# A post-norm layer on one core: the order of work ahead of its branch and in its closing stretch

## The chip, the cores and the metric

The kernel runs on one core of a Trainium2 chip. The core has a matrix engine (TensorE, PE in the profile, with PEld for its weight loads), VectorE (DVE), ScalarE (ACT), GpSimd (POOL), SyncE (SP, which here only issues DMAs) and 16 DMA engines. The metric is the time of one execution in device microseconds; the median of three runs is what the change is compared with.

## The reference

The input is x, 4 batches of 2048 tokens of 256 values. A gated linear attention of 16 heads (64 wide) and then a small "coupled" feed-forward follow, each with a residual and a layer norm.

```python
xn = _layer_norm(x, ln_gamma, ln_beta)
Q, K, V = xn @ WQ.T + bQ, xn @ WK.T + bK, xn @ WV.T + bV
gate = silu(xn @ Wg.T + bg);  alpha = sigmoid(alpha_logit)
h = alpha * h + k[:, None] * v[None, :];  o = q @ h          # step by step over the tokens, per head
x = layernorm(x + (x + (o * gate) @ WO.T + bO))

gf = global_net(x.mean(axis=1))                              # one number per batch
out = x
for _ in range(3):                                           # cycles 0, 1, 2
    tf = coupling_net(out)                                   # gelu, gelu, gelu, sigmoid; one number per token
    coupling = 0.1 + adaptive_range * (0.7 * gf + 0.3 * tf - 0.5) * 2
    out = out + coupling * twist(out)
x = layernorm(x + out)
```

`twist` permutes and negates quarters of a token's 256 values, and twisting twice gives the negative. So the kernel does not carry `out` through the cycles: it carries u = W1 applied to out and v = W1 applied to twist(out), and a cycle is u + c v and v - c u, with c the coupling of each token.

## The kernel before

**Stages.** First the constants are loaded and a few tables are made from the decay alpha: `up` and `down` (its powers, doubled step by step), `kf` and `qf` (what keys and queries are scaled by), `dtok` (decays by token), `bVt` (the bias of the values, repeated over the partitions). The first group of 512 tokens is normalised into `xn0` and its first values `V0` are made. A `flag` says whether the decays and weights lie in a safe range. Every engine reads the flag (line 1329) and branches: `program(True)` is the fast program, which these inputs take.

**The fast program** works through 4 batches of 4 groups of 512 tokens (`its` adds 8 head pairs to each). For each head pair it projects K, Q and gate, forms scores, updates of the state and products; between these pieces the function `between` slips in steps of three queues: `posts` (output projection and norm of a finished group), `nets` (the global net) and `couples` (the coupled feed-forward of two groups). A step is one piece of a Python generator, up to its next `yield step(...)`, with an engine and an estimated time that serve only to choose what is slipped in.

**Order on the engines.** The first stage and the fast program stand inside `tc.manual_schedule(engines=ORDERED)`: PE, DVE, ACT and POOL execute in the order in which the Python code issues, each on its own queue, and wait on each other through semaphores. What the last batch still has open after the last head pair is run by `the_end()`, which reads `AT_THE_END` letter by letter: `o` is the next step of a post, `n` of the global net, `p` of the couple of groups 0 and 1, `q` of the couple of groups 2 and 3, and `v` of `first_twisted`, which makes v for that second couple.

**The first stage around the change.** `double(i)` (VectorE) needs `powers[0]`, the sigmoid of the logit (ACT, line 257). In program order the doublings 0 to 2 stand between the statistics and the normalisation `xh` of the first group (line 159); the transposes of xh (line 182) and ACT's copies into `xn0` (line 184) follow, then the values (`values_of`: two matmuls, line 199, and an add on VectorE, line 203). The flag needs the largest of several squares, one of which is of the largest value of wQ (`peak`, line 295, a reduction of 128x2048 on VectorE), by way of `high`, `most`, `small`, `good`, and a matmul with ones (line 308). Values 3, two groups of transposes and ACT's two copies into `dtok` (line 324) end the stage. A PSUM bank there is one of four (`bank`).

**A couple's steps in the last batch** are: the first layer (line 823), layer 2 (line 905), layer 3 (line 940), layer 4 and tanh into `cs` (lines 949 and 952). Then for cycles 1 and 2 and for both halves s: `turn`, which scales `cs` into c (line 868), sends its first row through DRAM to get c by token (`by_token`, SP's DMAs), and updates; `gelu` (line 899) and layer 2; then layers 3 and 4. After cycle 2 the last tanh is by token (lines 957 and 959), the output's coefficients are worked out on VectorE with one power on POOL (lines 970 to 993), and the output is made by ACT (`own`, line 1002) and VectorE (`twisted`, line 1016) and stored.

In cycle 1 of the last batch VectorE and POOL share the update: VectorE makes c v (line 875) and adds it into u (line 878), POOL makes c u (line 876) and subtracts it from v (line 880):

```python
for o, (t0, t1) in enumerate(ts):
    nc.vector.tensor_mul(t0, cs[s], v[s][:, o, :])
    nc.gpsimd.tensor_mul(t1, cs[s], u[s][:, o, :])
```

`SPARE` holds four 128x512 buffers for each couple, which are no longer in use by then (a half of the values for the first, the tiles A and carry for the second). Cycle 2 uses VectorE alone and updates u only.

Of the kernel before, what the change touches and what calls it, by code (L numbers as in the profile page):

```python
# [42 lines left out]
F32 = mybir.dt.float32  # L43
I32 = mybir.dt.int32
U8 = mybir.dt.uint8
AF = mybir.ActivationFunctionType
# [23 lines left out]

AT_THE_END = "qoopooqnnqnpqppvppqvqqqpqppqqpqqpqppqpppppqqqpqpqqqqpqpqpppqqpqpppqpppqqqpqqqqqq"
STAGES = ((2, 4), (8, 4), (32, 2))
# [6 lines left out]
def post_norm_layer(ctx: ExitStack, tc: tile.TileContext, a: dict, out: bass.AP):  # L79
# [152 lines left out]
    with ExitStack() as first:  # L232
# [4 lines left out]
        def bank():  # L237
            return psum.tile([P, 512], F32, tag="pf", name="pf")


        diag = work.tile([P, HP, P], F32, tag="diag", name="diag")
# [13 lines left out]
        nc.vector.memset(high, 0.0)  # L255
        powers = [work.tile([P, HP, 1], F32, tag=f"apow{i}", name="apow") for i in range(C.bit_length())]
        nc.scalar.activation(powers[0], logit.unsqueeze(2), AF.Sigmoid)

# [32 lines left out]
        square(4, w_in["K"].rearrange("p k o -> p (k o)"))  # L291
        values_of(bank(), xn0, V0, 0, 0)

# [4 lines left out]
        nc.vector.tensor_mul(high[:, 5:6], peak, peak)  # L298
        values_of(bank(), xn0, V0, 0, 1)
        most = work.tile([P, 1], F32, tag="most", name="most")  # L300
# [4 lines left out]
        nc.vector.scalar_tensor_tensor(good, low, LOW_ALPHA, small, ALU.is_ge, ALU.mult)  # L305
        values_of(bank(), xn0, V0, 0, 2)
        pt = bank()
        nc.tensor.matmul(pt[0:1, 0:1], good, ones[:, 0:1], start=True, stop=True)
# [6 lines left out]
        values_of(bank(), xn0, V0, 0, 3)  # L315
        for half in range(2):
            hps = slice(half * (HP // 2), (half + 1) * (HP // 2))
            pt = bank()
            for j in range(HP // 2):
                nc.tensor.transpose(  # L320
                    pt[:, j * P : (j + 1) * P],
                    two[:, half * (HP // 2) + j].rearrange("p c s -> p (c s)"), ident,
                )
            nc.scalar.copy(dtok[:, hps, :].rearrange("p j i -> p (j i)"), pt)  # L324

# [9 lines left out]
    def layer(fast, inside):  # L335
# [335 lines left out]
        def step(kind, time, ready=always, act=0.0, delay=0.0, at=None):  # L671
            return kind, time, ready, act, delay, at
# [111 lines left out]
        def feed_forward(b, g0):  # L784
# [20 lines left out]
            u, v = [], []  # L805
            h1, h2 = {}, {}
            done = {}

# [52 lines left out]
            def first_twisted():  # L861
                for s in range(2):
                    yield from first(s, w1j, v, "v")

            def turn(s, cycle):

                yield step("dve", 0.75, lambda: b in shift and len(v) == 2, at=lambda: max(done["cs"], shift[b][1]))
                nc.vector.tensor_scalar(cs[s], cs[s], ar3, shift[b][0], ALU.mult, ALU.add)
                by_token(s, cycle - 1)
                if cycle == 1 and end:  # L870

                    done["u", s] = yield step("dve", 2.6)
                    ts = [(new("t"), SPARE[g0].pop(0)) for o in range(2)]
                    for o, (t0, t1) in enumerate(ts):
                        nc.vector.tensor_mul(t0, cs[s], v[s][:, o, :])
                        nc.gpsimd.tensor_mul(t1, cs[s], u[s][:, o, :])
                    for o, (t0, t1) in enumerate(ts):
                        nc.vector.tensor_add(u[s][:, o, :], u[s][:, o, :], t0)
                    for o, (t0, t1) in enumerate(ts):
                        nc.gpsimd.tensor_sub(v[s][:, o, :], v[s][:, o, :], t1)  # L880
                    return
                for o in range(2):
                    done["u", s] = yield step("dve", 1.3)
                    uo, vo = u[s][:, o, :], v[s][:, o, :]
                    t0 = new("t")
                    nc.vector.tensor_mul(t0, cs[s], vo)
                    if cycle == 1:
                        t1 = new("t")
                        nc.vector.tensor_mul(t1, cs[s], uo)
                        done["u", s] = yield step("dve", 1.3)  # L890
                    nc.vector.tensor_add(uo, uo, t0)
                    if cycle == 1:
                        nc.vector.tensor_sub(vo, vo, t1)

            def gelu(s):
                done["h1", s] = yield step("act", 1.4, delay=0.2, at=lambda: done["u", s])
                for o in range(2):
                    h1[s, o] = new("h1")
                    nc.scalar.activation(h1[s, o], u[s][:, o, :], AF.Gelu, bias=b1[:, o : o + 1])

# [22 lines left out]
            for cycle in range(3):  # L923
                if cycle and end:
                    for s in range(2):
                        yield from turn(s, cycle)
                    for s in range(2):
                        yield from gelu(s)
                        yield from layer2(s)
                elif cycle:  # L930
                    for s in range(2):
                        yield from turn(s, cycle)
                        yield from gelu(s)
# [433 lines left out]
```

## Time and profile before

| what | value |
|---|---|
| median of three runs | 1835.79 us (1835.6 to 1835.98) |
| the profiled execution | 1836.18 us, of which the span is 1834.4 us |
| TensorE busy | 1781.6 us, 97% of the span |
| VectorE busy | 1348.1 us, 73% |
| ScalarE busy | 755.7 us, 41% |
| GpSimd busy | 499.5 us, 27% |
| mean granted TensorE clock | 0.994 |
| first projection of the fast program (line 480) | begins at 24.97 us |
| last matmul of the program (line 957) | 1817.79 us and 1.05 us |
| last VectorE instruction | begins at 1829.07 us |

The profile is of one execution. A line such as `L878 DVE TENSOR_TENSOR u<-u,t 128x512 f32<-128x512 f32 x4 | 6.9, 1755 | 0.0` names the line of the kernel, the engine, the operation, the tile written and those read, the shape, the number of instructions, then their busy time in microseconds, the mean of one in nanoseconds and the idle time before them. The chain of work that ended last is followed back from the end: each piece is what released the next one. A window row gives the stretch, its length, the busy time of PE, PEld, VectorE, ACT and POOL with their instructions, the granted clock of TensorE, the share of the DMA engines and GB/s.

### The profile page before, as it was taken

The page shows a single profiled execution, that of the slowest core. Times are in us where ns is not written, and L with a number is a line of the kernel's source. Part 1 is how long each engine was busy: PE and PEld are TensorE (multiplying, and loading weights), DVE is VectorE, ACT ScalarE, POOL GpSimd, SP SyncE. Part 2 cuts the span into 40 slices and gives each one's busy share as a digit, 9 for nine tenths or more (in the row PEclk, how much of TensorE's full clock was granted, in tenths as well). Part 3 has the DMA queues.
Part 4 walks back from the last instruction along what each step waited for, and adds up shares of the span by engine and source line. Part 5 has one row for each costly group of instructions (what it writes and reads, how often), then busy time and mean ns, then how long its engine had stood idle before and what let it go on. Part 6 is the DMA issues. An engine that isn't in the chain of part 4 may idle for free.

```text
span 1834.4 us, 47983 instructions
## 1 busy us (share of the span) xinstructions
PE 1781.6 (97%) x20894; PEld 1026.4 (56%) x20894; DVE 1348.1 (73%) x3099; ACT 755.7 (41%) x1226; POOL 499.5 (27%) x452
## 2 busy tenths in 40 slices
PE   7999999999999999999999999999999999999985
PEld 3655555566555555565555555565555555555541
DVE  5677775767887868877688776877668876777467
ACT  3222324322454434543354334553355433453545
POOL 1332232223233222233132222222222232222242
PEclk9999999999999999999999999999999999999997
DMA  4000000000001000010001100010000100000002
GB/s 166 2 2 25 2 25 2 1 25 2 25 14 36 24 13 13 25 36 14 24 2 36 36 2 25 2 48 25 1 25 2 47 25 2 2 4 22 24 2 60
DMA packets 43819, 39.69 MB, mean 22 GB/s; under 512 B 20912, under 2 KB 39216, under 8 KB 43600
## 3 DMA queue, kind: packets, MB, share of 16 engines
q1 hardware_dynamic: 42320, 36.25, 6.2%
q8 instruction: 166, 2.72, 0.6%
q14 instruction: 53, 0.43, 0.1%
q10 hardware_dynamic: 1280, 0.29, 0.1%
HBM read 21.26 MB, written 15.27 MB: 20 GB/s over the span
## 4 chain that ended last, share of the span: by engine, by line
PE 89%; DVE 9%; issue 1%; ACT 1%; DMA 0%; POOL 0%; DVEq 0%; ACTq 0%
PE pj L480 34%; PE pj L683 12%; PE pj L199 11%; PE sc L573 4%; PE pj L905 4%; PE pu L1144 4%; PE pu L1161 4%; PE pj L630 4%; PE pj L847 3%; PE sc L646 3%; PE pj L940 1%; DVE states L656 1%; PE pj L823 1%; PE pj L949 1%; PE pj L710 1%
## 5 line engine op out<-in xcount | busy, mean ns | idle before, releaser
L526 POOL TENSOR_TENSOR qd<-QA,up 128x512 f32<-128x512 f32 x128 | 164.3, 1284 | 1159.6 <-ACT QA L498 1107.5
L494 ACT ACTIVATE KT<-pj,bK 128x512 f32<-128x512 f32 x128 | 87.9, 687 | 471.2 <-PE pj L480 471.2
L480 PE MATMUL pj<-xn,wK 128*128 128x512 f32 x512 | 253.8, 618 | 0.8 <-ACT dtok L324 0.8
L480 PE MATMUL pj<-xn,wg 128*128 128x512 f32 x512 | 240.6, 592 | 0.0
L480 PE MATMUL pj<-xn,wQ 128*128 128x512 f32 x512 | 240.6, 592 | 0.0
L656 DVE SCALAR_TENSOR_TENSOR states<-states,up,sc 128x64 f32<-128x64 f32 x768 | 215.8, 281 | 27.4
L199 PE MATMUL pj<-wV,xn 128*128 128x512 f32 x496 | 233.4, 593 | 0.0
L683 PE MATMUL pj<-wO,og 128*128 128x256 f32 x1024 | 231.9, 379 | 1.5 <-DVE og L1174 1.5
L683 PEld LDWEIGHTS pj<-wO,og 128*128 128x128 f32 x1024 | 194.3, 190 | 54.2 <-issue 27.7
L635 DVE TENSOR_TENSOR KE<-pj,dtok 128x512 f32<-128x512 f32 x128 | 88.1, 689 | 175.5 <-PE pj L630 175.5
L536 POOL TENSOR_TENSOR QF<-QA,qf 128x512 f32<-128x512 f32 x128 | 175.0, 1367 | 0.0
L480 PEld LDWEIGHTS pj<-xn,wQ 128*128 128x128 f32 x512 | 97.3, 190 | 122.4 <-issue 120.8
L480 PEld LDWEIGHTS pj<-xn,wg 128*128 128x128 f32 x512 | 97.3, 190 | 122.4 <-issue 110.2
L589 ACT COPY A<-sc 32x256 f32<-32x256 f32 x256 | 92.4, 361 | 147.0 <-PE sc L573 143.8
L498 ACT ACTIVATE QA<-pj,bQ 128x512 f32<-128x512 f32 x128 | 87.9, 687 | 140.5 <-PE pj L480 140.5
L480 PEld LDWEIGHTS pj<-xn,wK 128*128 128x128 f32 x512 | 86.7, 189 | 70.7 <-issue 62.2
L1161 PEld LDWEIGHTS pu<-A,V 64*64 64x64 f32 x4096 | 71.4, 134 | 84.9 <-DVE A L594 41.2
L199 PEld LDWEIGHTS pj<-wV,xn 128*128 128x128 f32 x496 | 84.6, 191 | 59.3 <-issue 59.3
L729 DVE TENSOR_TENSOR X<-pj,X 128x512 f32<-128x512 f32 x66 | 45.4, 688 | 96.9 <-PE pj L683 96.9
L510 ACT ACTIVATE gate<-pj,bg 128x512 f32<-128x512 f32 x128 | 88.0, 688 | 67.2 <-PE pj L480 62.7
L1174 DVE TENSOR_TENSOR og<-pu,gate 64x256 f32<-64x256 f32 x256 | 108.0, 422 | 6.3
L203 DVE TENSOR_TENSOR V<-pj,bVt 128x512 f32<-128x512 f32 x124 | 85.3, 688 | 34.4 <-PE pj L199 34.1
(222 smaller groups left out, 2721.2 us busy)
## 6 DMA issues: line engine op xcount, KB each, us to landing
X<-in_x SPq DMA_DIRECT2D x15, 512.0 KB, 3.8
out<-y SPq DMA_DIRECT2D x28, 256.0 KB, 2.1
kept<-X SPq DMA_DIRECT2D x13, 512.0 KB
x<-kept SPq DMA_DIRECT2D x13, 512.0 KB, 3.4
wV<-in_WV SPq DMA_DIRECT2D x1, 1024.0 KB, 6.2
wK<-in_WK SPq DMA_DIRECT2D x1, 1024.0 KB
wQ<-in_WQ SPq DMA_DIRECT2D x1, 1024.0 KB, 6.6
wg<-in_Wg SPq DMA_DIRECT2D x1, 1024.0 KB
```

Of the source, the lines that this page charges most:

```text
L199: nc.tensor.matmul(ps, xnT[:, k, i * P : (i + 1) * P], w_in["V"][:, k, half * 512 : (half + 1) * 512], start=(k == 0), stop=(k == KD - 1),)
L480: nc.tensor.matmul(ps, w_in[n][:, k, hp * P : (hp + 1) * P], xn[b, g][:, k, :], start=(k == 0), stop=(k == KD - 1),)
L494: nc.scalar.activation(kt, ps, AF.Identity, bias=b_in["K"][:, hp : hp + 1])
L510: nc.scalar.activation(gt, ps, AF.Silu, bias=b_in["g"][:, hp : hp + 1])
L526: nc.gpsimd.tensor_mul(qd, QA[it][:, :, 0:C], up[:, it[2], 1 : C + 1].unsqueeze(1).to_broadcast([P, NC, C]))
L536: nc.gpsimd.tensor_mul(qs[:, :, 0:C].rearrange("p c (n l) -> p c n l", l=H), qv.rearrange("p c (n l) -> p c n l", l=H), qf[:, hp, :].unsqu ...
L589: nc.scalar.copy(av[r, :, H:], pv[r, :, C : C + H])
L635: nc.vector.tensor_mul(ke, pt.rearrange("p (i x) -> p i x", i=NT), at(dtok, it[2], [P, NT, P]))
L656: nc.vector.scalar_tensor_tensor(o, before, up[:, hp, C : C + 1], u, ALU.mult, ALU.add)
L683: nc.tensor.matmul(ps[:, ii * D : (ii + 1) * D], og[b, g, hp][:, i * P : (i + 1) * P], wO[:, hp, :], start=(hp == hps[0]), stop=(hp == hps ...
L1161: tc.keep_in_program_order(nc.tensor.matmul(po[place(h, c), c, i * C : (i + 1) * C], V[r, i, m + h, :], A[r, h, i, :], start=False, stop=T ...
L1174: nc.vector.tensor_mul(ov[r, 1], pv[place(h, 1), 1], gv[r, 1])
```

## The change

Ahead of the branch:

- The sigmoid is the first instruction of the stage (ahead of the `diag` product and the copies into `bVt`).
- The adds and matmuls of values 1 stand with those of values 0, ahead of `peak`.
- The transposes and copies that make `dtok` stand ahead of the flag's matmul. The flag, `kf`, `qf` and values 3 follow.

In cycle 1 of the last batch:

- `turn` makes a new u in a `SPARE` buffer on VectorE alone: c v, then that plus u. POOL has no part in it. From then on `u_of` gives the new buffer.
- `turn_v`, a new step on VectorE behind layer 2 of both halves, multiplies the old u by c in its place and subtracts it from v.
- `AT_THE_END` lists the steps anew; it has two more `p` and two more `q`, for `turn_v`.

```diff
+        powers = [work.tile([P, HP, 1], F32, tag=f"apow{i}", name="apow") for i in range(C.bit_length())]
+        nc.scalar.activation(powers[0], logit.unsqueeze(2), AF.Sigmoid)
         diag = work.tile([P, HP, P], F32, tag="diag", name="diag")
...
-        powers = [work.tile([P, HP, 1], F32, tag=f"apow{i}", name="apow") for i in range(C.bit_length())]
-        nc.scalar.activation(powers[0], logit.unsqueeze(2), AF.Sigmoid)
...
-        values_of(bank(), xn0, V0, 0, 0)
+        for i in range(2):
+            values_of(bank(), xn0, V0, 0, i)
         peak = work.tile([P, 1], F32, tag="peak", name="peak")
...
-        values_of(bank(), xn0, V0, 0, 1)
...
         values_of(bank(), xn0, V0, 0, 2)
-        pt = bank()
-        nc.tensor.matmul(pt[0:1, 0:1], good, ones[:, 0:1], start=True, stop=True)
-        nc.vector.tensor_scalar(flag, pt[0:1, 0:1], P - 0.5, None, ALU.is_ge)
-
-        nc.vector.tensor_copy(kf[:, :, 0 : M + 1], down[:, :, C - M : C + 1])
-        nc.vector.tensor_copy(qf[:, :, M:H], up[:, :, 0:M])
-        nc.vector.reciprocal(kf[:, :, M + 1 : H], up[:, :, 1:M])
-        nc.vector.reciprocal(qf[:, :, 0:M], down[:, :, C - M : C])
-        values_of(bank(), xn0, V0, 0, 3)
         for half in range(2):
...
             nc.scalar.copy(dtok[:, hps, :].rearrange("p j i -> p (j i)"), pt)
+        pt = bank()
+        nc.tensor.matmul(pt[0:1, 0:1], good, ones[:, 0:1], start=True, stop=True)
+        nc.vector.tensor_scalar(flag, pt[0:1, 0:1], P - 0.5, None, ALU.is_ge)
+
...
+        values_of(bank(), xn0, V0, 0, 3)
...
-AT_THE_END = "qoopooqnnqnpqppvppqvqqqpqppqqpqqpqppqpppppqqqpqpqqqqpqpqpppqqpqpppqpppqqqpqqqqqq"
+AT_THE_END = "qoovoqonnpnppqpppvqpqpqpppqqpqqqpppqpppqppqpqqpqpqqqqpqqqpqpqqpqpqpqppqpppqpqqqqqqqq"
...
+            def u_of(s, o):
+                return new_u.get((s, o), u[s][:, o, :])
...
-                    done["u", s] = yield step("dve", 2.6)
-                    ts = [(new("t"), SPARE[g0].pop(0)) for o in range(2)]
-                    for o, (t0, t1) in enumerate(ts):
-                        nc.vector.tensor_mul(t0, cs[s], v[s][:, o, :])
-                        nc.gpsimd.tensor_mul(t1, cs[s], u[s][:, o, :])
-                    for o, (t0, t1) in enumerate(ts):
-                        nc.vector.tensor_add(u[s][:, o, :], u[s][:, o, :], t0)
-                    for o, (t0, t1) in enumerate(ts):
-                        nc.gpsimd.tensor_sub(v[s][:, o, :], v[s][:, o, :], t1)
+                    done["u", s] = yield step("dve", 2.8)
+                    for o in range(2):
+                        new_u[s, o] = SPARE[g0].pop(0)
+                        nc.vector.tensor_mul(new_u[s, o], cs[s], v[s][:, o, :])
+                        nc.vector.tensor_add(new_u[s, o], new_u[s, o], u[s][:, o, :])
                     return
...
+            def turn_v(s):
+
+                yield step("dve", 2.8)
+                for o in range(2):
+                    uo, vo = u[s][:, o, :], v[s][:, o, :]
+                    nc.vector.tensor_mul(uo, uo, cs[s])
+                    nc.vector.tensor_sub(vo, vo, uo)
...
                     for s in range(2):
                         yield from gelu(s)
                         yield from layer2(s)
+                    if cycle == 1:
+                        for s in range(2):
+                            yield from turn_v(s)
```

In steps, from the point where p's `cs` of cycle 0 is at hand, the new list runs: u of p; between its pieces the first layer of q; layer 2 of q and p; v of p; u of q; cycle 2 of p; v of q; cycle 2 of q; the coefficients and outputs of p and q.

More of the change, by code (lines that the diff above doesn't have):

```diff
@@ L324, in post_norm_layer @@
             nc.scalar.copy(dtok[:, hps, :].rearrange("p j i -> p (j i)"), pt)
+        pt = bank()
+        nc.tensor.matmul(pt[0:1, 0:1], good, ones[:, 0:1], start=True, stop=True)
+        nc.vector.tensor_scalar(flag, pt[0:1, 0:1], P - 0.5, None, ALU.is_ge)
+        nc.vector.tensor_copy(kf[:, :, 0 : M + 1], down[:, :, C - M : C + 1])
+        nc.vector.tensor_copy(qf[:, :, M:H], up[:, :, 0:M])
+        nc.vector.reciprocal(kf[:, :, M + 1 : H], up[:, :, 1:M])
+        nc.vector.reciprocal(qf[:, :, 0:M], down[:, :, C - M : C])
+        values_of(bank(), xn0, V0, 0, 3)
         nc.gpsimd.iota(trow, pattern=[[1, C]], base=0, channel_multiplier=0)
@@ L806, in feed_forward @@
             h1, h2 = {}, {}
+            new_u = {}
             done = {}
@@ L883, in turn @@
                     done["u", s] = yield step("dve", 1.3)
-                    uo, vo = u[s][:, o, :], v[s][:, o, :]
+                    uo, vo = u_of(s, o), v[s][:, o, :]
                     t0 = new("t")
@@ L898, in gelu @@
                     h1[s, o] = new("h1")
-                    nc.scalar.activation(h1[s, o], u[s][:, o, :], AF.Gelu, bias=b1[:, o : o + 1])
+                    nc.scalar.activation(h1[s, o], u_of(s, o), AF.Gelu, bias=b1[:, o : o + 1])
+            def turn_v(s):
[4 more added lines that the diff above has]
+                    nc.vector.tensor_sub(vo, vo, uo)
             def layer2(s):
```

## The prediction

> **What bounds the kernel now.** I read the chain of work that ended last first, because it says which stages can pay at all. On the page its shares are:
>
> ```profile
> PE 89%; DVE 9%; issue 1%; ACT 1%; DMA 0%; POOL 0%; DVEq 0%; ACTq 0%
> ```
>
> The long middle belongs to TensorE (PE) and its instruction stream is not touched. The change lies in the two ends, so I read those in the trace. For the first 45 us, the chain in order of time (start, length, engine and line; "xh" is the normalised X):
>
> ```profile
> 9.03 1.28 ACT L257
> 10.32 0.22 ACT apow L257
> 10.57 0.17 DVE up L262
> ...
> 11.66 0.33 DVE xh L159
> ...
> 17.64 2.20 DVE peak L295
> ...
> 24.71 0.18 ACT dtok L324
> 24.97 5.39 PE pj L480 x12
> ```
>
> The reader should see three things: a table load and the sigmoid hold VectorE (DVE) up to 10.57, since the doublings precede xh in its order (the wait rows give 2.8 us of idle there, released by apow); the reduction of wQ leads to the flag; and the first projection of the branch waits for the second dtok copy, which ends at 24.87.
>
> For the end I took busy time by window (length, PE, PEld, DVE, ACT, POOL, then the granted clock):
>
> ```profile
> 1770.00:1780.00 10.00, 9.88 (x26) 3.34 (x24) 9.97 (x7) 5.53 (x10) 9.26 (x7) 1.00 0.06 2
> 1780.00:1790.00 10.00, 6.06 (x11) 1.76 (x12) 9.97 (x8) 4.46 (x7) 9.64 (x6) 0.88 0.03 0
> 1790.00:1800.00 10.00, 7.36 (x14) 2.12 (x14) 8.53 (x9) 4.21 (x7) 6.82 (x5) 0.67 0.03 1
> 1800.00:1810.00 10.00, 7.83 (x20) 2.45 (x17) 9.35 (x16) 6.99 (x11) 0.00 (x0) 0.94 0.24 54
> ```
>
> From 1770 VectorE is the full engine, with 7 or 8 instructions in 10 us; when POOL (GpSimd) is silent it does 16. The groups by shape, first 1768.2 to 1797.3 (cycle 1, POOL working), then 1797.3 to 1811 (cycle 2, POOL idle):
>
> ```profile
> L878 DVE TENSOR_TENSOR u<-u,t 128x512 f32<-128x512 f32 x4 | 6.9, 1755 | 0.0
> L868 DVE TENSOR_SCALAR cs<-cs,ar,sh 128x512 f32<-128x512 f32 x4 | 5.0, 1253 | 0.0
> L875 DVE TENSOR_TENSOR t<-cs,v 128x512 f32<-128x512 f32 x4 | 4.7, 1226 | 0.1
> ```
>
> ```profile
> L891 DVE TENSOR_TENSOR u<-u,t 128x512 f32<-128x512 f32 x4 | 2.8, 692 | 0.1
> L868 DVE TENSOR_SCALAR cs<-cs,ar,sh 128x512 f32<-128x512 f32 x4 | 2.2, 544 | 1.6 <-ACT cs L952 1.6
> L886 DVE TENSOR_TENSOR t<-cs,v 128x512 f32<-128x512 f32 x4 | 2.8, 688 | 0.1
> ```
>
> Same forms, 2.5 times the time: the add goes from 692 to 1755 ns, the scale from 544 to 1253. What differs between the stretches is POOL, 9.6 of 10 us busy in one and 0 in the other. So I read the end as VectorE and POOL holding each other up.
>
> The sum is made against the profiled execution: 1836.18 us, of which 1834.4 span and 1.78 around it. The median shown, 1835.79, lies 0.39 lower; I take that off last. All times below are positions in the old trace.
>
> **First stage, step by step.**
> - *Sigmoid first.* ScalarE (ACT) issues its DMAs until 4.71, then has a table load at 4.75 to 6.03, the bVt copies at 6.72 and 8.43, a second load at 9.03 and the sigmoid at 10.32. With the sigmoid first, one 1.28 us load should serve both. The sigmoid waits for logit, issued at 1.67 on ACT's queue: it cannot be later than 10.32; the nearest rows are X's half before it on that queue (landed 6.39) and bg behind it (4.27 + 4.3 = 8.6). The copies now queue behind it, but the values that need bVt come at 14.4, so that is free. VectorE has finished its statistics at 7.77, POOL's power ends at 8.94, so xh starts near 9.0 instead of 11.58: 2.58 us earlier (1.7 if logit lands at 8.6). The four squares (1.3 us) move ahead of the xn copies and end at 10.35, before xn at 10.62.
> - *Values 1 ahead of the flag.* VectorE must now add values 1 before it reduces wQ. In the old trace their matmuls end near 18.62 (the weight loads that follow show it), shifted 16.04; values 0 are added by 15.06. So VectorE idles 1 us and then adds (0.61 start to start), and peak starts at 16.65 instead of 17.56. From there by the old distances: peak 2.31, high 0.18, most 0.18, small 0.19, good 0.07, add of values 2 0.60: flag at 20.18 instead of 21.59, 1.41 earlier. wQ (issued 7.46, 6.6 us to landing) is there by 14.1. The cover at risk is TensorE's first clock: these matmuls start at half pace (loads 0.85 us apart until 15.68, 0.43 from 16.32). All fast or all slow, values 1 end at 14.7 or 18.0, and the flag at 19.1 or 22.2.
> - *Decays ahead of the flag.* Eight transposes (1.04) fill TensorE's idle before the flag matmul (it waited 0.88 there), from 17.8 to 18.8, against good at 19.6: free. Their two copies (1.07) leave the end of ACT's queue. Last is now VectorE's add of values 3: flag 20.18, the two copies and two reciprocals (flag to that add: 1.96 old), add 22.14 to 22.76. Old: copy until 24.87, projection at 24.97; new: near 22.86. TensorE, POOL and ACT read the flag in about 0.5 us at their sequencers (TENSOR_LOAD rows), done by 21, so the branch is covered; should it not be, VectorE's own 0.55 us load is the bound.
> - Sum: 2.1 us earlier into a stream that TensorE bounds, so it keeps to the end. SP's loads run to 28 in both and its next, X2, serves work tens of us later. Bounds: 0 (values 1 late) to 2.95 (the projection waits only for TensorE, 22.0). I take 2.1, from the middle pace as the old rows had it.
>
> **The end, step by step.** Per couple, cycle 1 loses 8 POOL instructions (4 multiplies of 1.63 to 1.75, 4 subtractions of 1.71) and VectorE goes from 8 to 16 (4 multiply-add pairs into new_u, then 4 multiply-subtract pairs for v). With POOL silent I price them from cycle 2: start to start scale 0.57, independent 0.61, dependent 0.72. So scale and u of one group cost 3.24 (1797.43 to 1800.67 shows it), v of one group 2.66.
> - *Start.* The order puts q's v matmuls (3.44) ahead of the transposes that feed the global net, and p's L949 (1.06) between its second and third step, but takes q's second u (3.6) out of it. Followed by rows: transposes end 1761.95, x1T 1762.9, net 1763.7 to 1766.45, tg 1767.4, first scale 1767.94 against 1768.27.
> - *VectorE's list from there*, in the listed order: u of p 6.48 (to 1774.4); v of p 5.32 (1779.7); q's scale waits for its tanh, 0.8 (TensorE: u 1769.9, v 1773.3, two L905 1776.8, L940 1777.8, h3, L949 1779.75, tanh 1780.5); u of q 6.48 (1787.0); cycle 2 of p 6.48 (1793.5); v of q 5.32 (1798.8); cycle 2 of q 6.48 (1805.3). TensorE and ACT fit between: p's second tanh ends 1786.7 and q's is needed at 1798.8, its matmul ready at 1796.3. That tanh reuses the cs buffers that v of q reads, so its second half waits until 1798.2 on ACT, with p's h3 and token tanh behind it (done 1800.6, needed 1805.3) and q's first gelu (1800.9): covered. If that cover went, each us of it would cost one.
> - *Output.* p's coefficients start at 1805.3, not 1813.68. ACT's first output 4.29 later, 1809.6, holds q's last h3 until 1810.7; then 0.7, the token matmuls and tanh 1.2, and 0.3: q's coefficients at 1812.85. Old 1819.66; from there everything to the end is the same 9.8 us of VectorE and 5 us of store: 6.8 earlier.
> - *SP.* Row DMAs stay two per scale, but earlier. The load of the kept x waited for the u buffer (1803.53); v of p frees it by 1777. In the worst place, behind q's last row at 1804.4, it lands 3.4 later at 1807.8, against 1809.6.
> - *TensorE's clock.* It fell about 2 us into a gap: idle from 1785.54, and
>
> ```profile
> 1787.50:1788.00 0.50, 0.00 (x0) 0.00 (x0) 0.50 (x1) 0.49 (x1) 0.50 (x1) 0.61 0.00 0
> ```
>
> then L905 cost 3.45 us for 1.72. My schedule has gaps of about 2.4 and 2.6 us before 1802 and before q's last tokens. By the row both go slow: the first hides behind own (1.8 us of slack), the second costs 0.3. The Trainium skill (TensorE: Matmul & The Clock Gate, What's actually happening) puts the fall after an idle window of about 3.4 us; by that neither gap would, and the end would come 0.3 earlier. The trace fell sooner, so I take 6.5.
> - Bounds of the end: 8.4 (p's coefficients' whole gain, if q's tokens never wait) and 3 (VectorE's list held up 3.5 us by late tanh or gelu).
>
> **Rivals.**
> - *Order is the bound at the end*: two tanh or gelu arrive late because ACT takes them in listed order behind others, or slow-clock stretches (1.7 us per L905) fall on the chain. For: old PE windows show clock 0.67 and waits for L899. Against: then VectorE waited, now it has 5.3 us of v to fill. Gain 3.3 + 2.1: 1830.4.
> - *The first stage gives nothing*: half-pace values 1, flag at 22.2, only the end's 6.5: 1829.3.
> - *Both*: 1832.5, which is within 0.2% (about 3.7 us) of before, about what a measurement of this kernel can tell.
> - *Slower*: VectorE's long instructions were not POOL's doing but the end's own traffic (ACT and TensorE reading the same tiles). Then the 32 instructions of u and v stay dear: at the old mean of 1.49 they cost 26 us more than at 0.67, and the end comes 19 us later, near 1853. It decides at 0.87 us apiece (6.5 over 32 on top of 0.67), 0.94 with the first stage counted in. Against: cycle 2 has that traffic too and 0.69. The Trainium skill (GPSIMD Engine Reference, Specifications) says the two engines share SBUF interfaces and contend when VectorE has two SBUF inputs or a two-port mode; that speaks against this rival, and the rows agree (0.69 to 1.75).
>
> **How the numbers follow.** Forecast 1836.18 - 2.1 - 6.5 - 0.39 = 1827.2. Chances: forecast 0.62, order 0.13, first stage nothing 0.13, both 0.08, slower 0.04. All but the last two are faster by over 0.2%, plus some of "both": 0.90; same 0.06; slower 0.04. Low end: 2.95 + 8.4 gives 1824.4, a little under for the token wait; high end: "both" at 1832.
>
> **What would show it.** One table load before the sigmoid, xh near 9, flag near 20.2, first L480 near 22.9; in the end no 128x512 work on POOL, VectorE's tensor_tensor at 0.69 throughout, no wait over 1 us in its list, and 37.4 us from the first scale to p's coefficients where it was 45.4. Wrong if VectorE waits for tanh more than 2 us in the list, if u instructions stay over 0.9, or if the flag is not earlier.

## The result and the profile after

The changed kernel takes 1829.33 us (median of six runs, 1827.72 to 1830.27); the kernel before took 1835.88 us beside it (1835.53 to 1836.33). The ratio is 0.9964, with a 95% interval of 0.9954 to 0.9974: 6.55 us faster, 2.1 us less gain than forecast. The profiled execution took 1830.14 us, of which 1828.0 us are the span. It is one of the slower of the six: the changed kernel spreads over 2.6 us where the kernel before spread over 0.8.

The chain of work that ended last, by engine, has the shape it had:

```profile
PE 90%; DVE 9%; issue 1%; ACT 0%; DMA 0%; POOL 0%; DVEq 0%; ACTq 0%; POOLq 0%
```

The first 45 us of that chain in order of time (start, length, engine, tile and line):

```profile
9.00 0.42 DVE xh L159
...
9.47 1.97 PE pf L182 x8
11.44 4.75 PE pf L199 x8
...
16.21 0.69 DVE V L203
16.90 2.20 DVE peak L296
...
23.29 5.38 PE pj L480 x12
```

The sigmoid, its table load and the doublings are gone from the chain: xh begins at 9.00 where it began at 11.58, as forecast. Before `peak` there are now 6.7 us of TensorE (the transposes and the matmuls of values 0 and 1; the profile counts each of these four matmuls of the code as two) and the add of values 1. The first projection begins at 23.28, not 24.97.

At the end, the busy time by window (length, PE, PEld, VectorE, ACT, POOL, granted clock):

```profile
1770.00:1780.00 10.00, 9.19 (x25) 3.27 (x23) 9.04 (x15) 6.61 (x11) 0.00 (x0) 1.00 0.19 53
...
1790.00:1800.00 10.00, 7.37 (x27) 2.72 (x26) 9.72 (x16) 6.02 (x11) 0.00 (x0) 0.95 0.03 1
1800.00:1810.00 10.00, 8.22 (x10) 2.49 (x10) 6.06 (x24) 3.61 (x7) 1.64 (x1) 0.54 0.05 1
```

Up to 1800 VectorE executes 15 or 16 instructions in 10 us where it executed 7 to 9, and POOL has nothing. The last row is the surprise: TensorE's granted clock is 0.54. By shape, 1766.5 to 1803.9:

```profile
L872 DVE TENSOR_SCALAR cs<-cs,ar,sh 128x512 f32<-128x512 f32 x8 | 4.3, 543 | 0.7 <-ACT cs L963 0.7
...
L880 DVE TENSOR_TENSOR V<-V,u 128x512 f32<-128x512 f32 x4 | 2.8, 692 | 0.1
```

The add that took 1755 ns takes 692, the scale 543 for 1253 (the multiplies, in rows not shown, take 684 to 689). The only wait of size in the list is 0.7 us for q's tanh.

To compare kernels, the span is cut at four instructions: the first projection (line 480), the shift of the global net (`sh`, which the first scale follows 0.26 us later), and the first instruction of p's and of q's coefficients. All in us, read from the start of those instructions in the profiled executions:

| kernel | flag | first projection | shift | shift to p's coefficients | p's to q's | q's to end | span |
|---|---|---|---|---|---|---|---|
| before | 21.59 | 24.97 | 1768.01 | 45.67 | 5.98 | 14.72 | 1834.4 |
| after | 20.45 | 23.28 | 1766.32 | 37.59 | 9.42 | 14.66 | 1828.0 |

The 6.4 us of span are 1.7 at the shift, 8.1 up to p's coefficients, less 3.4 between p's and q's. The last of these was forecast as 1.9 (1.57 and 0.3).

### The profile page after: what moved, and what is told of

It reads as the page before. It is cut to its first block, busy times and chain, and to the rows that moved or that the text cites. A ratio compares the mean times of both kernels' runs of the same rounds, so it can differ in the third digit from the quotient of the medians.

```text
span 1828.0 us, 47958 instructions
## 1 busy us (share of the span) xinstructions
PE 1779.4 (97%) x20894; PEld 1027.0 (56%) x20894; DVE 1343.8 (74%) x3115; ACT 753.9 (41%) x1225; POOL 473.0 (26%) x436
## 4 chain that ended last, share of the span: by engine, by line
PE 90%; DVE 9%; issue 1%; ACT 0%; DMA 0%; POOL 0%; DVEq 0%; ACTq 0%; POOLq 0%
PE pj L480 34%; PE pj L683 12%; PE pj L199 11%; PE sc L573 4%; PE pj L913 4%; PE pu L1155 4%; PE pu L1172 4%; PE pj L630 4%; PE pj L848 3%; PE sc L646 3%; PE pj L824 2%; PE pj L951 1%; DVE states L656 1%; PE pj L960 1%; PE pj L710 1%; PE pj L182 1%
```

## The experiments

Times are medians; each ratio is to the kernel before on the same chip (1835.48 to 1835.89 us). The columns on the right are cut as above, each in one profiled execution.

| kernel | us (range, runs) | ratio, 95% | flag | first projection | shift to p's | p's to q's |
|---|---|---|---|---|---|---|
| e1, first stage alone | 1833.74 (1832.33 to 1836.21, 11) | 0.9989, 0.998 to 0.9998 | 20.37 | 23.20 | 45.36 | 5.97 |
| e2, end alone | 1829.72 (1829.33 to 1831.25, 6) | 0.9966, 0.9954 to 0.9979 | 22.03 | 25.41 | 37.58 | 8.76 |
| e3, VectorE alone, old order | 1827.66 (1827.12 to 1828.15, 5) | 0.9955, 0.9941 to 0.9969 | 21.81 | 25.19 | 37.07 | 5.97 |
| e4, after with POOL at work | 1843.91 (1 run) | | 18.87 | 21.70 | 52.72 | 9.68 |
| e5, after with filled gaps | 1827.56 (1826.22 to 1828.06, 5) | 0.9953, 0.9939 to 0.9966 | 19.99 | 22.82 | 37.57 | 7.39 |
| f1, e3 with the new first stage | 1824.95 (1824.78 to 1826.91, 5) | 0.9945, 0.9931 to 0.9958 | 18.66 | 21.49 | 37.07 | 5.97 |
| f2, e3 with the sigmoid first | 1825.31 (1824.83 to 1827.17, 5) | 0.9945, 0.9931 to 0.9958 | 18.61 | 23.61 | 37.07 | 5.97 |
| f3, f1 with values 1 put back | 1825.10 (1824.75 to 1825.62, 5) | 0.9943, 0.9929 to 0.9956 | 18.75 | 21.58 | 37.07 | 5.97 |
| g1, e5 with multiplies and adds apart | 1826.07 (1825.52 to 1828.77, 5) | 0.9952, 0.9938 to 0.9966 | 18.79 | 21.62 | 36.59 | 7.57 |
| g2, g1 with values 1 put back | 1825.74 (1825.18 to 1826.37, 5) | 0.9946, 0.9932 to 0.9959 | 18.27 | 21.10 | 36.60 | 7.56 |

### Each half alone (e1, e2)

e1 is the kernel before with the changed first stage and nothing else, e2 the kernel before with the changed end and the new list. In e1, for instance:

```diff
+        powers = [work.tile([P, HP, 1], F32, tag=f"apow{i}", name="apow") for i in range(C.bit_length())]
+        nc.scalar.activation(powers[0], logit.unsqueeze(2), AF.Sigmoid)
...
-        values_of(bank(), xn0, V0, 0, 0)
+        for i in range(2):
+            values_of(bank(), xn0, V0, 0, i)
```

> The kernel before with only the first stage changed (sigmoid, values 1 and decays moved). Theory: the first projection begins 1.7 us earlier, as in the changed kernel, and since TensorE bounds the middle, nearly all of it is still there at the end: 1.2 to 1.7 us faster, the runs as close together as those of before. Rival (a shift at the start is swallowed later, and the whole gain is the end's): within 0.4 us of before.

> The kernel before with only the end changed. Theory: 5 to 6.5 us faster, the runs spread over 2 us or more as those of the changed kernel are, since the spread comes from TensorE's clock in the last cycle; the VectorE list from first scale to the first couple's coefficients 37.3 us. Rival (the spread comes from the first stage): the same mean gain, the runs within 0.6 us.

The first stage alone gives 2.0 us, the end alone 6.1. Together they would be 8.1, and the changed kernel has 6.55. Both halves help, so the rivals in which one of them gives nothing fall, but the missing 1.5 us is not explained by the halves. The same end took 8.76 us from p's to q's coefficients in e2's profile and 9.42 in the changed kernel's, so 0.7 of it may lie there. The executions of kernels with the new first stage also spread by 2 to 4 us (e1 from 1832.33 to 1836.21), where e1 was expected to be as steady as before, and that spread became a question of its own, below. e2 spreads by 1.9, but by one execution alone: the profiled one took 1831.25, the other five 1829.33 to 1830.03, so its 8.76 need not hold for them.

### Whose doing were the long instructions, and what is the new order worth? (e3, e4)

e3 is the kernel before with its list, its buffers and its order, but POOL's sixteen instructions on VectorE:

```diff
-                        nc.gpsimd.tensor_mul(t1, cs[s], u[s][:, o, :])
+                        nc.vector.tensor_mul(t1, cs[s], u[s][:, o, :])
...
-                        nc.gpsimd.tensor_sub(v[s][:, o, :], v[s][:, o, :], t1)
+                        nc.vector.tensor_sub(v[s][:, o, :], v[s][:, o, :], t1)
```

> The kernel before, its list and first stage as they were, with the 16 GpSimd multiplies and subtractions of cycle 1 issued on VectorE in the same places. Theory (GpSimd and VectorE hold each other up): VectorE then needs 0.57 + 8 x 0.66 = 5.9 us for each of the four turns instead of 7.1, so it comes out 3 to 5 us faster although VectorE has 16 instructions more. Rival 1 (the gain of the end comes from u being first, not from GpSimd's absence): 0 to 1 us faster. Rival 2 (VectorE's long instructions are not GpSimd's doing): 32 instructions at 1.5 us, 20 us slower.

e4 does the opposite: it is the changed kernel with sixteen unrelated multiplies on POOL, which read `cs` and a weight and write into a weight that is no longer used. Nothing waits for their results.

```diff
                         nc.vector.tensor_add(new_u[s, o], new_u[s, o], u[s][:, o, :])
+                    for o in range(4):
+                        nc.gpsimd.tensor_mul(
+                            w_in["Q"][:, o // 2, o % 2 * G : (o % 2 + 1) * G], cs[s], w_in["K"][:, o // 2, o % 2 * G : (o % 2 + 1) * G]
+                        )
```

> The changed kernel with 16 multiplies of 128x512 added on GpSimd in cycle 1, four per turn, reading cs and a weight that is no longer used and writing another such weight; nobody waits for them. Theory (the two engines slow each other whatever data they work on): VectorE's instructions beside them take 1.2 to 1.75 us instead of 0.69, its list grows by 10 to 16 us and the whole by about as much. Rival (VectorE was slowed in the kernel before by its waits for what GpSimd produced, not by GpSimd being busy): under 1 us slower.

The groups of e4 by shape, 1764 to 1817.5, first VectorE's and then POOL's:

```profile
L880 DVE TENSOR_TENSOR V<-V,u 128x512 f32<-128x512 f32 x4 | 6.6, 1641 | 0.1
...
L911 DVE TENSOR_TENSOR v<-v,u 128x512 f32<-128x512 f32 x4 | 2.8, 692 | 0.1
```

```profile
L882 POOL TENSOR_TENSOR wQ<-cs,wK 128x512 f32<-128x512 f32 x16 | 27.0, 1717 | 17.9 <-DVE cs L872 17.9
```

The same adds go back from 692 to 1641 ns with nothing else changed on VectorE, and the subtractions that run while POOL is silent (line 911) stay at 692. Sixteen POOL instructions make the stretch from the shift to p's coefficients 15.1 us longer (52.72 for 37.59). So the long instructions were POOL's doing, and the rival of the end's own traffic is refuted.

e3 says the rest. In the old order, VectorE alone reaches p's coefficients 8.6 us earlier than before (37.07 for 45.67), and q's come 5.97 behind as they always did. It is 1.7 us faster than the changed kernel by the medians, although it has none of the first stage's gain. The last two windows of e3 up to 1810:

```profile
1790.00:1800.00 10.00, 7.83 (x19) 2.49 (x19) 9.52 (x16) 7.47 (x12) 0.00 (x0) 1.00 0.20 54
1800.00:1810.00 10.00, 8.41 (x30) 3.12 (x28) 5.69 (x23) 5.77 (x10) 1.64 (x1) 1.00 0.05 1
```

TensorE has more than 7.8 us of work in each, and its clock stays at 1.00 (from 1770 to 1790 as well). Taking POOL out is thus the whole gain of the end: e3 has 8.1 us, more than the 3 to 5 expected of it, and with the new order (e2) it is 2.1 us less.

### What the new order costs: the clock (e5)

In the changed kernel, between p's cycle 2 and q's coefficients, this is what the two engines do (start, length, engine, line, tiles, and in brackets the idle time before and what ended it):

```profile
1800.39 3.78 PE L913 MATMUL pj<-h,w 128*128 128x512 f32 x4 [0.97 <-ACT h L899]
...
1803.91 0.29 DVE L981 TENSOR_SCALAR c<-c,ar,sh 128x8 f32<-128x8 f32 x1
...
1805.56 3.76 PE L913 MATMUL pj<-h,w 128*128 128x512 f32 x4 [1.39 <-ACT h L899]
...
1807.99 0.17 DVE L1004 TENSOR_TENSOR base<-nb,mj 128x8 f32<-128x8 f32 x1
...
1809.36 0.69 ACT L915 ACTIVATE h<-pj,b 128x512 f32<-128x512 f32 x1 [3.24 <-PE pj L913]
1809.94 1.08 ACT L1013 ACTIVATE y<-x,base,a 128x256 f32<-128x256 f32 x2
...
1813.34 0.29 DVE L981 TENSOR_SCALAR c<-c,ar,sh 128x8 f32<-128x8 f32 x1 [1.64 <-ACT c L970]
```

and the clock beside it, from the windows of 2 us:

```profile
1798.00:1800.00 2.00, 1.23 (x8) 1.14 (x8) 1.96 (x3) 0.68 (x3) 0.00 (x0) 0.73 0.00 1
...
1806.00:1808.00 2.00, 2.00 (x3) 0.73 (x3) 0.43 (x4) 0.11 (x1) 1.47 (x1) 0.50 0.00 0
1808.00:1810.00 2.00, 2.00 (x4) 0.19 (x2) 0.15 (x1) 0.65 (x2) 0.00 (x0) 0.71 0.00 0
```

In the 2 us before, TensorE worked 0.52 us at 1.00. The clock falls to 0.50 near 1798.9 (0.73 over 2 us is 1.08 us at half) and comes back near 1809.2. So not one but both layer-2 groups of q take 3.8 us for 1.9. The second is what counts: ACT takes its work in listed order, and `h` of q (line 915), which waits 3.24 us for that group, stands ahead of p's output (line 1013). The output's inputs were ready at 1808.16; it began at 1809.94.

e5 is the changed kernel with six matmuls whose result nobody reads, put into TensorE's gaps: in cycle 2, two behind p's layer 3 (line 951), one behind p's token matmuls and three behind q's first layer-2 group.

```diff
+            def fill(n):
+                for i in range(n):
+                    nc.tensor.matmul(pj(), w2[:, 0, :], w_in["K"][:, 0, 0:512], start=True, stop=True)
...
-                        yield from layer2(s)
+                        yield from layer2(s, 3 if second and cycle == 2 and s == 0 else 0)
...
+                if end and not second and cycle == 2:
+                    fill(2)
...
+                    if end and not second:
+                        fill(1)
```

> The changed kernel with six unread 128x128 by 128x512 products on TensorE in three gaps of the last cycle: two behind the first couple's L951, one behind its L968, three behind the second couple's first layer 2. Theory (the output waits because TensorE runs at half clock from 1799 to 1809): the clock stays at 1.00 there, layer 2 takes 1.9 us instead of 3.8, the second couple's coefficients follow the first's by 7.7 us instead of 9.4; 1.5 to 2 us faster than the changed kernel's slower runs, median near 1827.7, spread under 1 us. Rival (the output waits for ACT's listed order): the same time as the changed kernel or up to 0.5 us more.

In e5 the window from 1800 (those beside it have 1.00 too), and then q's second layer-2 group (line 917 there) and p's first output (line 1022 there), read:

```profile
1800.00:1805.00 5.00, 4.80 (x11) 1.85 (x11) 4.79 (x18) 2.74 (x4) 0.00 (x0) 1.00 0.08 1
```

```profile
1804.60 1.88 PE L917 MATMUL pj<-h,w 128*128 128x512 f32 x4
...
1807.69 1.09 ACT L1022 ACTIVATE y<-x,base,a 128x256 f32<-128x256 f32 x2 [0.48 <-DVE base L1013]
```

The clock stays at 1.00, the group takes 1.88, p's output begins 4.28 us after p's coefficients (the forecast had 4.29; after had 6.03), and q's coefficients come 7.39 after p's instead of 9.42. That is 2.0 us for six useless matmuls, 1.8 by the medians of the two kernels. The rival of ACT's order is only half wrong: the order is what passes TensorE's delay on to p's output, but without the slow clock it costs nothing here. The spread did not shrink to the 1 us expected (1826.22 to 1828.06); the first stage, below, has a part in it.

### What is left of the order: pairs (g1, g2)

e5 still needs 44.96 us from the shift to q's coefficients, where e3 needs 43.04. One difference is how multiply and add follow each other. The first group of the changed kernel and of e3 on VectorE, after:

```profile
1767.16 0.69 DVE L879 TENSOR_TENSOR V<-cs,v 128x512 f32<-128x512 f32 x1
1767.89 0.69 DVE L880 TENSOR_TENSOR V<-V,u 128x512 f32<-128x512 f32 x1
1768.50 0.68 DVE L879 TENSOR_TENSOR V<-cs,v 128x512 f32<-128x512 f32 x1
```

and e3:

```profile
1769.18 0.69 DVE L875 TENSOR_TENSOR t<-cs,v 128x512 f32<-128x512 f32 x1
1769.79 0.68 DVE L876 TENSOR_TENSOR V<-cs,u 128x512 f32<-128x512 f32 x1
```

An instruction that needs the one just before it starts 0.72 or 0.73 behind it, one that does not 0.60 or 0.61. It is the need that counts and not the step from multiply to add: e3's first add, at 1771.59, starts 0.60 behind a multiply that it does not need. The old code makes all multiplies of a half first. g1 gives the new list the same habit:

```diff
                         nc.vector.tensor_mul(new_u[s, o], cs[s], v[s][:, o, :])
+                    for o in range(2):
                         nc.vector.tensor_add(new_u[s, o], new_u[s, o], u[s][:, o, :])
...
                     nc.vector.tensor_mul(uo, uo, cs[s])
-                    nc.vector.tensor_sub(vo, vo, uo)
+                for o in range(2):
+                    nc.vector.tensor_sub(v[s][:, o, :], v[s][:, o, :], u[s][:, o, :])
```

> The changed kernel with the six filling products, and in the two updates of cycle 1 both multiplies ahead of both adds (or subtractions), so that no instruction follows the one that it needs. Theory (on VectorE an instruction that needs the one before it starts 0.72 us after it, any other 0.60): 16 pairs save 0.12 us each, so the time from the shift to the first couple's coefficients falls from 37.6 to 35.7 us, as far as the tanh do not come later than VectorE is ready; 0.5 to 1.9 us faster than with the filling products alone, near 1826.2. Rival (the tanh set the pace): under 0.3 us faster.

g2 is g1 with the add of values 1 behind `peak` again, as before the change.

> The same with values 1 back behind the reduction of wQ: the new list without what was found against it. Theory (the newly listed order is worth nothing of its own): within 1 us of the old list with all on VectorE and the same first stage (1825.1). Rival (u first is worth something once TensorE's clock and the pairs are mended): 1823.5 or less.

In g1 the stretch from the shift to p's coefficients is 36.59 for e5's 37.57: 0.98 us, as eight pairs at 0.12 would give. Sixteen pairs were set apart, and 35.7 us had been expected: the eight of p earn nothing, because q's first scale then waits 1.69 us for its tanh instead of 0.69 (from the shift to that scale both kernels need 12.83); the eight of q earn the 0.98. Its median is 1.5 below e5's; the first stage has a share in that which the medians do not part from it (the flag came 1.2 us earlier in g1's profile than in e5's, with the same code). The sum to q's coefficients is now 44.16, still 1.1 behind e3's 43.04. Even filled and spread out, the new list only approaches the old one: g2 and f3 have the same first stage and stand at 1825.74 and 1825.10. Their ranges do not exclude a tie (1825.18 to 1826.37, 1824.75 to 1825.62), and against the kernel before on its own chip (1835.89 and 1835.48) the two gain 10.2 and 10.4 us, so I take from it that the new list has no worth of its own, not that it must be worse.

### Which part of the first stage pays (f1, f2, f3)

These three put parts of the first stage on e3, whose end took the same 37.07 and 5.97 us in all three. f1 is all of it; f2 moves only the sigmoid; f3 is f1 without the step that sets values 1 ahead of `peak`:

```diff
-        for i in range(2):
-            values_of(bank(), xn0, V0, 0, i)
+        values_of(bank(), xn0, V0, 0, 0)
...
+        values_of(bank(), xn0, V0, 0, 1)
```

> The whole changed first stage, and at the end the old list with GpSimd's work issued on VectorE. Theory (the newly listed order brings nothing beyond the move to VectorE, and costs what TensorE's clock costs): first projection near 23.2, the second couple's coefficients 6.0 us after the first's; 1.7 to 2 us faster than the same end with the old first stage, about 1825.8, and some 3.5 us faster than the changed kernel. Rival (the new order and the earlier start need each other): as fast as the changed kernel, 1828 or more.

> Of the first stage only the sigmoid is moved; the end is the old list with everything on VectorE. Theory (the sigmoid makes the whole gain, and values 1 ahead of the reduction cost part of it): flag near 19.1, dtok copies to 22.3, first projection near 22.4, so 0.8 us earlier than with all three moves; near 1825. Rival (all three moves are needed): first projection 24 or later, 1826.5 or more.

> Sigmoid and decays moved, values 1 back behind the reduction; the end is the old list with everything on VectorE. Theory (values 1 cost the flag the time that VectorE idles for them and the add): flag near 19.1, first projection near 22.0, 1.2 us earlier than with all three moves; near 1824.6, the fastest of all. Rival (values 1 are hidden where they stand): first projection within 0.3 us of that with all three moves.

From e3's 1827.66 the medians go to 1824.95, 1825.31 and 1825.10: 2.7, 2.4 and 2.6 us (2.4, 2.0 and 2.3 if each is set against the kernel before on its own chip, 1835.48 for the three and 1835.78 for e3). The sigmoid alone has nearly all of it, and by medians nothing can be told between the three. In the profiled executions something can. f2's first projection began at 23.61 (22.4 expected), 2.0 us behind f3's. TensorE had nearly nothing to do ahead of the flag (0.14 us from 16 to 18 us), its granted clock fell (0.84 over the next 2 us, 0.50 from 20 to 22) and it worked slowly: values 3 took 2.82 us, and the transposes for the decays (f2, start and length)

```profile
20.98 1.91 PE L321 MATMUL pf<-ident,two 128*128 128x128 f32 x8
```

In f3 values 3 took 1.98 and the eight transposes, standing ahead of the flag, 1.04: 1.7 of the 2.0 us. So moving the decays does a second thing that was not in the forecast: it keeps TensorE at work. That is one execution of f2 (1826.25 us, above its median), and the size of it in the median is not shown.

Values 1 ahead of `peak` bring nothing and, in these profiles, cost nothing: f3's first projection is within 0.1 us of f1's, as the rival had it, and not 1.2 us ahead. Putting them back moves the median by +0.15 us (f1 to f3) and -0.33 (g1 to g2), and the range of the five executions narrows from 2.1 to 0.9 and from 3.3 to 1.2. In f3 `peak` waits for wQ instead:

```profile
14.71 2.29 DVE L295 TENSOR_REDUCE peak<-wQ 128x1 f32<-128x2048 f32 x1 [1.30 <-DMA wQ<-in_WQ]
```

So when TensorE is fast, values 1 are added at 14.31 (f1) and `peak` begins at 15.01, 0.3 behind the wait for wQ. When it is slow, they are added at 16.21 (after) and `peak` at 16.82. This order ties the flag to TensorE's pace.

**The pace of the first stage.** after, e1, e4, e5, f1 and g1 have the same instructions up to the flag. The same eight transposes read, in after and then in f1:

```profile
9.47 1.97 PE L182 MATMUL pf<-ident,xh 128*128 128x128 f32 x8 [1.07 <-DVE xh L159]
```

```profile
9.16 1.41 PE L182 MATMUL pf<-ident,xh 128*128 128x128 f32 x8 [1.01 <-DVE xh L159]
```

The twelve matmuls (as the profile counts them) of values 0 to 2 behind them take 6.65 and 5.42 us. after, e1 and e5 have 1.97 us for the transposes and the flag at 20.45, 20.37 and 19.99; f1, e4 and g1 have 1.41 and the flag at 18.66, 18.87 and 18.79. Same code, 1.1 to 1.8 us apart. It is TensorE's clock. The trace's record of the granted clock starts only at 13.8 us in after and at 7.9 in f1, and a window row reads 1.00 where there is no record yet, so the rows of that stretch do not tell the two apart. Where the record starts is a first sign: ahead of the transposes in the three fast traces (7.5 to 9.0 us), behind them in the three slow ones (12.9 to 14.0). The weight loads of the values are a second: in after they follow each other by 0.85 us up to 13.11 and by 0.43 from 13.87, in f1 by 0.43 from 11.11 on. In e3 the record reaches back far enough: the same eight transposes, at 11.58, take 1.97 us there, and beside them stands

```profile
12.00:13.00 1.00, 1.00 (x7) 1.00 (x6) 0.97 (x7) 0.26 (x1) 0.00 (x0) 0.50 1.03 422
```

In all traces with the old first stage (before, e2, e3) xh comes later (transposes from 11.58 to 12.04), and they took 1.97. The times of before and e3 vary by 1.1 us at most, so the new first stage does not only start earlier, it can also meet either clock. Why the clock is up in some executions by then and not in others is not shown.

### The best version

f1 and f3, the old list and buffers with VectorE alone at the end, and the new first stage (f3 without its step on values 1), beat both kernels: f3 stands at 1825.10 us, 10.4 below the kernel before and 4.2 below the changed one (3.8 if each is set against the kernel before beside it). f3 is the better choice of the two by its range of 0.9 us against 2.1, in five executions each; f2, with the sigmoid alone, is as fast by the median.

## Why the prediction was right and wrong

The direction and the main mechanisms were right, one step failed (below), the gain came out a quarter smaller (6.55 of 8.6 us by the medians), and 1829.33 lies inside the range. It also lies where the rival "the first stage gives nothing" was put (1829.3), by coincidence: the first stage gave 1.7 of its 2.1 us in the profiled execution and 2.0 alone, and the end gave too little. The changed kernel's median alone could not have told this, since it lies only 0.4 below e2's.

- *Sigmoid first.* As forecast: one table load (4.76), logit landed in time for the sigmoid at 7.59, xh at 9.00 (9.0 forecast).
- *Values 1 ahead of the flag.* The middle pace was assumed and the trace had it: `peak` at 16.82 (16.65), flag at 20.45 (20.18). Bounds for all fast and all slow (19.1 and 22.2) were the right thing to keep, though the lower one was too high: f1 came out at 18.66 with the same code. But the step itself, which the forecast credited with a share of the 2.1, earns nothing (f3). wQ lands later than the 14.1 that was read from the old rows, at 14.7 in f3, which did not matter at the middle pace.
- *Decays ahead of the flag.* Free for TensorE, as said. The last wait of the branch is then VectorE's add, at 22.41 (22.14), and 0.25 us more, which was missed: the first projection waits for a small cast (line 416) behind that add. It began at 23.28 for 22.86.
- *"It keeps to the end".* Not quite. The gain of 1.69 us is still 1.55 at 1319 us and 1.20 from 1336 us on (at the same instructions of line 594 in both traces). e1, f1 and f3 lose 0.3 to 0.55 likewise between the first projection and the shift. After ends that stretch even with before only because the new order brings the shift 0.45 earlier (e2), about the 0.33 that the step *Start* forecast. 0.35 of the loss lies in one place: at 1331.04 VectorE's instruction that writes u (line 853) waits 0.46 us for products of TensorE (line 1155), where in the kernel before it follows without a wait, and TensorE then waits 1.1 us instead of 0.8 for A (line 594). All eight kernels with the decays moved have this wait; before, e2, e3 and f2 do not. Why moving the decays brings it stays open.
- *The rival "slower"* asked whose doing the long instructions were. e3 and e4 answer it from both sides. The Trainium skill (GPSIMD Engine Reference, Specifications) says that GpSimd and VectorE contend for shared SBUF interfaces when VectorE has two SBUF inputs or is in a two-port mode, and the runs agree as far as they go: 692 to 1641 ns for the add (e4), 0.55 to 1.49 us for a single scale (before, where the mean of four is 1253 ns). That the interfaces are the cause, no run here shows.
- *VectorE's list.* From the first scale to p's coefficients 37.33 (37.4 forecast), with one wait of 0.69 (0.8). The single terms (0.57, 0.61 and 0.72) all held. *SP* was covered as said: the kept x was issued at 1775.84.
- *Output, and the step that failed.* The failed step is "TensorE's clock": "By the row both go slow: the first hides behind own (1.8 us of slack), the second costs 0.3." I priced each gap as one slow group and let the clock recover between them. It stayed at half for 10.2 us, over both groups of q's layer 2: the 3.78 us of the first did not bring it back. This is the slow-clock half of the rival "order is the bound"; its late tanh and gelu did not come. And the cover was not there: the second group's gelu stands *ahead* of p's output in ACT's order, so p's output moved with it (6.03 after the coefficients, 4.29 forecast), and the token matmuls behind it, too. q's coefficients came 9.42 after p's; 7.55 and 0.3 had been forecast. e5 confirms the size by taking the cause away: 7.39.
- *The page against the row.* The Trainium skill (TensorE: Matmul & The Clock Gate, What's actually happening) would have the clock fall after about 3.4 us of idleness. Here it fell 2.4 us after the last large matmuls ended (1796.5 to 1798.9), and eight tiny ones had begun 0.7 us before the fall. The row was the better guide, and by the page's rule the forecast would have been further off.

The sum against the profiled executions: forecast 8.56 us (2.1, 0.33, 8.0, less 1.57 and 0.3), measured 6.38. The missing 2.2 are 0.4 at the first projection, 0.3 between there and the shift, and 1.6 between p's and q's coefficients; the 8.08 from the shift to p's coefficients met the 8.0. The profiled execution of after is 0.8 above its own median. Besides, 2.14 us of it lie outside the span, where the kernel before has 1.78; the other five executions of after have 2.1 to 2.2 there too, so some 0.35 us of the gain are lost outside the span, which the forecast had put at nothing.

What was also wrong is a thing the prediction did not ask: whether the new list was needed at all. It priced "POOL out" and "new order" as one; done apart, the first gives 8.1 us (e3) and the second takes 2.1 of them (e2).

## What to carry to other kernels

When two engines share the data of one stage, measure each one's instruction with the other silent before splitting the work: here one engine alone does it faster than both together, in the old order and with two words changed. Where TensorE has gaps of a few microseconds, follow the clock past the gap, through every group until enough work has restored it, and look in the consumer's listed order for what stands behind the slow group. If a list is rearranged along with another change, price the two apart.

## What the runs showed of the hardware that was not expected

- One POOL multiply (128x512, f32) in flight beside VectorE costs VectorE 0.9 us: 16 of them made the list 15.1 us longer (e4). They took 1717 ns themselves.
- On VectorE an instruction that reads the result of the one before it starts 0.72 to 0.73 us behind it, an independent one 0.60 to 0.61 (128x512, f32). Eight pairs set apart gave 0.98 us (g1, behind q's first scale).
- After the clock fell, 3.78 us of matmuls at 0.50 did not bring it back; it returned within the second such group, near 1809.2, 3.6 us into it. Between two changes of the granted clock there lie, in all twelve traces, 3.41 us or a whole multiple of it, and the half clock of after is three such stretches: TensorE worked 2.44 us in the first (from 1798.93), 2.03 in the second and all 3.41 in the third, at whose end the clock came back. In e3's first stage it worked 2.66 and then all of 3.41. Of all such stretches in the traces, the fullest that did not bring the clock back had 2.81 us of work (e2, from 11.20), the emptiest that did had 2.98 (before, from 1787.61). So a group of 3.78 us that is spread over two stretches need not bring it back. Six unread matmuls in the gaps kept it at 1.00 and were worth 2 us.
- The first matmuls of the same code run at one of two paces (transposes 1.97 or 1.41 us), with TensorE's clock at half or full, which moves the flag by 1.1 to 1.8 us from one execution to the next.
